# A graph network with a mixture of experts on one core: x by columns, staircases for four of 32 groups, and a unit product with a row of minus ones in the last stage

## Chip, core and metric

The kernel runs on one core of a Trainium2 chip, in one launch. The metric is the device time of that core in microseconds (us), the median of several runs. The core has five engines with one order of instructions each: TensorE (PE in the profile; PEld is its weight load), VectorE (DVE), ScalarE (ACT), GpSimd (POOL) and SyncE (SP), which here only issues transfers. Transfers run on 16 DMA engines.

## The reference

x has 6250 nodes of 256 numbers; 200,000 edges run from src to dst. With deg_out and deg_in, the numbers of edges that leave and enter a node (at least 1), the reference computes:

- h = x / sqrt(deg_out), summed over the edges into each dst, divided by sqrt(deg_in), then times W_gc plus b_gc, plus x times W_res plus b_res;
- a feed-forward network with 64 experts of which each node uses two (256 to 512 to 256, Gelu), weighted and added;
- a normalization over the nodes: subtract the mean of each column, divide by its deviation, times gamma, plus beta;
- x plus that, and a layer normalization over the 256 numbers of each node.

The first change touches deg_out and x times (W_gc, W_res), which are computed in one stage. The second touches the last two lines of this list.

## The kernel before

Nodes lie in 50 tiles of 125 rows (TP = 125, NT = 50). Edges lie in 1568 groups of 128, one edge in each partition.

**The degree stage** makes deg_out and the projections at once. Each src is split into a row (0 to 63, `row_b`) and a column (0 to 99, `col_b`). For a block of 32 groups VectorE builds one-hot tiles by comparison (`hot_pairs`, L250): `hot_row`, 64 wide, and `hot_col`, 100 wide, both bfloat16. For each group TensorE multiplies the one by the other and adds the result into the PSUM tile `degp` (L490), even groups into its upper half and odd groups into its lower half. After 49 blocks, `degp` holds the counts. They are copied to `dsb` (L518) and folded into one column per tile (`pd`, L521), from which `s_out`, one over the root of the degree, is made.

In each of the 49 turns TensorE also prepares one tile of nodes. `turned(t)` transposes the tile's two halves (L416) and ScalarE copies the result to `fT` (L419). `project(t)` multiplies `fT` by the joined weights (L425), and ScalarE copies the 512 columns to `hx` (L429). After each second tile SP writes half of `hx` to DRAM (`r_dram`, L166) and the other half into the large tile `hrow` (L164). x is loaded for two tiles at a time by `load`, two transfers for rows 0 to 111 and 112 to 124 (L164). Also in this stage SP writes zeros over `y_dram` (L453), ScalarE's queue writes zeros over `z_dram` (L507), ScalarE makes keys of the edges (`keyg`, L511), and VectorE does small pieces of the next stages (the table `masks`, L437 to L446).

The stage has its order written out by hand: each engine executes its instructions in the order of the program text. One turn issues `hot_row` and `hot_col` (two buffers each), then `turned(i + 1)`, then the 32 products, then `project(i)`, then zeros and keys. The tiles of PSUM and SBUF that are written in one turn have two buffers; the loaded x has three, of two tiles each.

**Between** lie the counting of edges per node and the sums over neighbours, the gathering of rows for sparse parts, the choice of experts, and the expert network. They aren't changed.

**The last stage** first adds the two experts' rows to x (L1528), with TensorE summing columns of x and of its squares (`pm` L1533, `pv` L1535). From these come `scale` and `less` (L1547), one row each, repeated in all partitions. `fb` holds x plus beta, loaded and added earlier. Then the 50 tiles go through in groups of 1, 2, 3, eight times 5, 3 and 1. For a group:

- `scaled`: VectorE multiplies x by `scale` (L1571) and subtracts `less` from `fb` (L1572). In a group of five it does that for three tiles only;
- `shifted`: for the other two tiles TensorE makes `fb` less `less` in PSUM, as a product of `fb` with the identity (L1564) plus a product of a row of minus ones with the row `less` (L1565). It is issued three groups ahead, with four PSUM buffers;
- `sums`: VectorE adds the two and sums each row (L1578), and scales the sums to minus means (L1580);
- `squares`: ScalarE sums the squares (L1587) and takes the root (L1589);
- `rows_out`, for the group before: VectorE finishes the factors (L1594, L1595) and makes the first output tile of a group of five (L1598), ScalarE makes the others (L1600), SP writes them out (L166).

Of the kernel before, what the change touches and what calls it, by code (L numbers as in the profile page):

```python
# [9 lines left out]
F32 = mybir.dt.float32  # L10
F32R = mybir.dt.float32r
BF16 = mybir.dt.bfloat16
# [4 lines left out]
ALU = mybir.AluOpType  # L17
# [129 lines left out]
def gnn_moe_kernel(ctx, tc, x_in, src, dst, bases, nexts, firsts, parts, lasts, W_gc, b_gc, W_res, b_res, Wg, bg, w1, b1, w2, b2,  # L147
# [68 lines left out]
    with tc.tile_pool(name="edges", bufs=1) as ep, ExitStack() as later:  # L216
# [46 lines left out]
        with tc.tile_pool(name="late", bufs=1) as lp, tc.tile_pool(name="both", bufs=2) as bp, \  # L263
# [145 lines left out]
            CG = 32  # L409
            degp = ps_deg.tile([128, 2 * NT], F32, name="degp")  # L410

            def turned(t):

                pt = ps_a.tile([128, 2, TP], F32, name="pt")
                for k in range(2):
                    T.transpose(pt[:, k, :], state[t - t % 2][:, t % 2, k * 128:(k + 1) * 128], ident[:TP, :TP])  # L416
                load(t + 4)
                state["fT", t] = ld.tile([128, 2, TP], F32, name="fT")
                S.copy(state["fT", t], pt)  # L419

            def project(t):

                pr = ps_a.tile([TP, 2 * D], F32, name="pr")
                for k in range(2):
                    T.matmul(pr, state["fT", t][:, k, :], wcat[:, k, :], start=(k == 0), stop=(k == 1))  # L425
# [30 lines left out]
            turned(0)  # L456
            for i in range(NGR // CG):
# [3 lines left out]
                hot_col = hp.tile([128, CG // 2, 2 * NT, 2], BF16, name="hot_col")  # L461
                hot_pairs(hot_col, col_b, c0, CG, 2 * NT)
# [24 lines left out]
                turned(i + 1)  # L487
                for c in range(CG):
                    r = c % 2
                    T.matmul(degp[64 * r:64 * r + 64, :], hot_row[:, c // 2, :, r],  # L490
                             hot_col[:, c // 2, :, r], start=(c0 + c < 2), stop=(c0 + c >= NGR - 2))
# [26 lines left out]
            V.tensor_copy(dsb, degp)  # L518
# [814 lines left out]
    fb = fpool.tile([TP, NT, D], F32, name="fb")  # L1333
# [4 lines left out]
    with tc.tile_pool(name="ex", bufs=2) as xp, \  # L1338
# [95 lines left out]
        def slotted():  # L1434
# [4 lines left out]
            for e in range(-1, E):  # L1439
# [20 lines left out]
                if e % 4 == 1 and e > 4 and e // 4 * 4 - 4 < NT:  # L1460
                    t0 = e // 4 * 4 - 4
                    n = min(4, NT - t0)
                    G.tensor_tensor(fb[:, t0:t0 + n, :], fb[:, t0:t0 + n, :],
# [47 lines left out]
    with tc.tile_pool(name="fin", bufs=1) as fp, tc.tile_pool(name="gat", bufs=8) as gp, \  # L1511
            tc.tile_pool(name="fl", bufs=2) as fl, \
            tc.tile_pool(name="ps_f", bufs=4, space=PSUM) as ps_f, \
# [43 lines left out]
        BY_PE = 2  # L1557

        def shifted(t0, n):
            if n < 5:  # L1560
                return
            pf = ps_f.tile([TP, BY_PE, D], F32, name="pf")
            for u in range(BY_PE):
                T.matmul(pf[:, u, :], ident[:TP, :TP], fb[:, t0 + n - BY_PE + u, :], start=True, stop=False)  # L1564
                T.matmul(pf[:, u, :], negs, less[0:1, :], start=False, stop=True)  # L1565
            part["pf", t0] = pf

        def scaled(t0, n):
            m = n - BY_PE if n == 5 else n
            xs, fs = x[:, t0:t0 + n, :], fb[:, t0:t0 + m, :]  # L1570
            V.tensor_tensor(xs, xs, scale[:, None, :].to_broadcast([TP, n, D]), ALU.mult)  # L1571
            V.tensor_tensor(fs, fs, less[:, None, :].to_broadcast([TP, m, D]), ALU.subtract)  # L1572

        def sums(t0, n):
            lm = fl.tile([TP, 5], F32, name="lm", bufs=3)
            for t in range(n):
                f = part["pf", t0][:, t - n + BY_PE, :] if n == 5 and t >= n - BY_PE else fb[:, t0 + t, :]
# [14 lines left out]
        def rows_out(t0, n):  # L1592
# [4 lines left out]
            if n == 5:  # L1597
                V.tensor_scalar(o[:, 0, :], x[:, t0, :], rs[:, 0:1], lm[:, 0:1], op0=ALU.mult, op1=ALU.add)  # L1598
            for t in range(int(n == 5), n):
# [3 lines left out]
        for g in groups[:4]:  # L1603
            shifted(*g)
        for i, g in enumerate(groups):
            if i + 4 < len(groups) and i:
                shifted(*groups[i + 3])
# [59 lines left out]
```

## Time and profile before

| | |
|---|---|
| median of the runs shown | 1617.59 us (3 runs, 1616.33 to 1620.51) |
| the profiled execution's own time | 1633.5 us |
| its span | 1631.8 us |
| mean granted clock of TensorE | 0.947 of full |
| TensorE busy | 1433.4 us (88%) |
| VectorE busy | 1077.0 us (66%) |
| ScalarE busy | 687.1 us (42%) |
| GpSimd busy | 778.6 us (48%) |
| degree products, first and last | 10.2 to 172.2 us of the span |
| last stage behind `less`, from | 1568.2 us of the span |

The profiled execution is 15.9 us longer than the median of the runs. Durations and the places in the span are read from it. In a timeline, the first two columns are the start and the length in us; "x4" says that four instructions are merged, and the brackets at the end tell how long the engine idled before and what ended that. In a table by windows, the columns are the window, its length, the busy time of PE, PEld, DVE, ACT and POOL with the number of instructions, the granted clock, the share of the DMA engines that was busy, and GB/s. In a table by groups, the numbers behind the first bar are the busy time in us and the mean ns of one.

### The profile page before, as it was taken

To read this page: it belongs to the slowest core of one execution; us is meant where nothing else is said; L and a number is where in the kernel's file an instruction comes from. 1 tells how busy PE (TensorE), PEld (TensorE's weight loads), DVE (VectorE), ACT (ScalarE), POOL (GpSimd) and SP (SyncE) were. 2 spreads that over 40 slices of the span, in tenths; PEclk is the share of its full clock that TensorE was granted. 3 is DMA by queue.
4 is the path that set the end of the run, shared out by engine and by line. 5 is a ranking of instruction groups with operands and counts; after the bars stand their busy time and mean duration, and the time that the engine had idled before them with its cause. 6 is when DMAs were issued, how large, how long until landed. Compare 5 with 4: busy or idle time off the path is not lost. (4 is left out here: it accounts for less than half of the span.)

```text
span 1631.8 us, 33437 instructions
## 1 busy us (share of the span) xinstructions
PE 1433.4 (88%) x10135; PEld 1176.7 (72%) x10135; DVE 1077.0 (66%) x2966; ACT 687.1 (42%) x1703; POOL 778.6 (48%) x878
## 2 busy tenths in 40 slices
PE   5999477888889999999999986699989999997993
PEld 3555366777778888989999975588778777775641
DVE  9999887878888878877777739533223222221897
ACT  2342543445555556555555533322122222122258
POOL 6000215666666666666666621256556666652000
PEclk9999799999999999999999997899999999999975
DMA  6889775667667777677777739488777878674924
GB/s 171 253 258 285 219 225 148 177 195 205 178 189 214 202 205 213 196 203 204 217 201 211 208 114 191 140 243 260 226 232 252 248 248 250 216 234 142 250 72 134
DMA packets 213271, 335.63 MB, mean 206 GB/s; under 512 B 23814, under 2 KB 148198, under 8 KB 213082
## 3 DMA queue, kind: packets, MB, share of 16 engines
q1 hardware_dynamic: 158294, 179.56, 38.0%
q0 software_dynamic: 47888, 146.77, 31.2%
q10 hardware_dynamic: 6900, 7.07, 1.5%
q8 instruction: 82, 1.34, 0.3%
q14 instruction: 107, 0.88, 0.2%
HBM read 253.81 MB, written 73.10 MB: 200 GB/s over the span
## 5 line engine op out<-in xcount | busy, mean ns | idle before, releaser
L568 POOL DMA_INDIRECT r<-h_dram,srcg x445 | 465.6, 1046 | 302.5 <-PE pc L651 108.8
L697 PE MATMUL sm<-hrow,counts 125*128 125x258 f32 x1500 | 496.2, 346 | 10.3 <-DVE counts L688 9.0
L671 ACT CAST counts<-pc 128x200 f32 (+7 forms) x879 | 360.9, 411 | 260.5 <-PE pc L651 135.5
L698 PE MATMUL sm<-hrow,counts 125*128 125x256 f32 x1500 | 402.4, 282 | 0.0
L651 PE MATMUL pc<-hotk,lo 128*128 128x250 bf16 (+7 forms) x1118 | 309.4, 308 | 60.7 <-DVE counts L688 22.3
L697 PEld LDWEIGHTS sm<-hrow,counts 125*128 125x128 f32 x1500 | 293.1, 195 | 35.8 <-issue 19.8
L638 DVE TENSOR_TENSOR hotk<-key,iota_h 128x800 bf16<-128x800 f16 (+4 forms) x488 | 250.8, 514 | 90.7 <-PE pc L651 56.1
L698 PEld LDWEIGHTS sm<-hrow,counts 125*128 125x128 f32 x1500 | 288.3, 192 | 1.6
L688 DVE TENSOR_TENSOR counts<-pc,counts 128x50 f32 x908 | 220.0, 242 | 57.3 <-issue 9.4
L1399 ACT ACTIVATE hT<-ph,b1c 128x112 f32<-128x112 f32 (+16 forms) x256 | 106.2, 428 | 349.1 <-PE ph L1397 183.7
L1409 PE MATMUL py<-w2s,hT 128*128 128x256 f32 (+7 forms) x992 | 240.4, 385 | 5.7 <-issue 4.0
L1397 PE MATMUL ph<-xgT,w1s 128*128 128x112 f32 (+17 forms) x1024 | 206.1, 345 | 8.7 <-ACT hT L1399 6.3
L1397 PEld LDWEIGHTS ph<-xgT,w1s 128*128 128x128 f32 x1024 | 169.4, 193 | 40.4 <-issue 12.9
L1409 PEld LDWEIGHTS py<-w2s,hT 128*128 128x128 f32 (+7 forms) x992 | 161.3, 171 | 50.2 <-issue 8.9
L1362 POOL DMA_INDIRECT y_dram<-ys,dest x124 | 119.2, 961 | 136.8 <-DVE ys L1412 70.0
L1362 POOL DMA_INDIRECT xg<-x_dram,ids x124 | 119.8, 966 | 91.8 <-DVE ids L1313 52.5
L1412 DVE TENSOR_TENSOR ys<-py,b2s 128x256 f32<-128x256 f32 (+7 forms) x124 | 51.6, 421 | 169.4 <-PE py L1409 112.4
L651 PEld LDWEIGHTS <-lo 128*128 128x128 bf16 x1118 | 101.6, 102 | 83.7 <-DVE lo L250 20.3
L573 PE MATMUL pg<-r,hot 128*128 128x258 f32 x445 | 147.3, 331 | 12.0 <-issue 7.1
L1387 DVE TENSOR_SCALAR xgT<-pte,bsum 128x112 f32<-128x112 f32 (+14 forms) x128 | 48.9, 424 | 159.7 <-PE pte L1384 65.1
L574 PE MATMUL pg<-r,hot 128*128 128x256 f32 x445 | 125.7, 282 | 0.0
L573 PEld LDWEIGHTS pg<-r,hot 128*128 128x128 f32 x445 | 85.8, 193 | 25.9 <-issue 18.6
(326 smaller groups left out, 1737.8 us busy)
## 6 DMA issues: line engine op xcount, KB each, us to landing
w1s<-in_L_gnn_w_dram SPq DMA_DIRECT2D x64, 512.0 KB
w2s<-in_L_gnn_w_dram SPq DMA_DIRECT2D x64, 512.0 KB
y_dram<-zeros SPq DMA_DIRECT2D x48, 256.0 KB
yr<-y_dram SPq DMA_DIRECT2D x25, 448.0 KB
b2s<-in_L_gnn_b_dram SPq DMA_DIRECT2D x64, 128.0 KB
r<-h_dram,srcg POOLq DMA_INDIRECT x445
h_dram<-hrow SPq DMA_DIRECT2D x5, 1344.0 KB
z_dram<-zeros ACTq DMA_DIRECT2D x7, 903.0 KB
```

The lines of the kernel that those rows point to most:

```text
L568: G.indirect_dma_start(out=f32(r[:, :2 * D]), out_offset=None, in_=h_dram[:, :], in_offset=bass.IndirectOffsetOnAxis(ap=idx, axis=0))
L573: T.matmul(pg, hot, r[:, D:], start=first, stop=False)
L574: T.matmul(pg[:, :D], hot, r[:, :D], start=False, stop=last)
L638: V.tensor_tensor(hot, pairs(key, e, n, m), iota_h[:, None, :m, :].to_broadcast([128, n // 2, m, 2]), ALU.is_equal)
L651: T.matmul(pc, los[g // PAIRS][:, r // 2, :, r % 2], hots.pop(g), start=(i == 0), stop=(i == k - 1))
L671: put = S.copy(counts[c % 2][:, :, 1:][:, :, ds(at, w - 1)], pc[:, :, 1:])
L688: add = V.tensor_tensor(to, more, f32(had), ALU.add).ins
L697: T.matmul(sm, by, hrow[:, t, D:], start=(t == 0), stop=False)
L698: T.matmul(sm[:, :D], by, hrow[:, t, :D], start=False, stop=(t == NT - 1))
L1362: w = G.indirect_dma_start(**kw)
L1397: T.matmul(ph[:, :m], w1s[:, kk, c * 128:(c + 1) * 128], xgT[:, kk, :m], start=(kk == 0), stop=(kk == 1))
L1409: T.matmul(py[:n], hT[:, c, k * 128:k * 128 + n], w2s[:, c, :], start=(c == 0), stop=(c == 3))
```

## The change

*Degree stage.* The host hands over a second copy of x, `x_cols`, laid out as pairs of tiles with columns in the partitions. `load` brings a pair with one transfer, straight as the stationary operand of the projection. `turned` is gone: no transposes, no `fT`. `load(t + 4)` is issued in `project(t)`, behind its products. `hot_col` is built for 28 of the 32 groups (CV = 28). For the other four ScalarE makes staircases: the sign of (column + 0.5 - j) for j from 0 to 100, that is 1 up to the column and -1 behind it, 101 values. Their products with `hot_row` add up in a second PSUM tile, `stp`. At the end the difference of neighbouring columns of `stp`, times 0.5, is added to `degp`: two VectorE instructions and a copy more. ScalarE makes the staircases for turn i + 1 in turn i, in front of the copy to `hx`; there are two buffers.

*Last stage.* A tile `unit` has the identity in rows 0 to 124 and minus ones in row 125. `fb` gets 128 partitions, and a transfer writes the row `less` into partition 125 of the forty tiles of the groups of five. One product of `unit` with 126 rows of `fb` then gives `fb` less `less`. It is done for all five tiles of such a group, so that `scaled` subtracts only in the small groups. `pf` has two buffers of five tiles (three PSUM banks each), and its products are issued one group ahead. VectorE makes two output tiles of a group of five instead of one, ScalarE three instead of four.

```diff
+            CV = CG - 4
+            stp = ps_deg.tile([128, 2 * NT + 1], F32, name="stp")
+            code = dp.tile([128, NGR // CG, CG - CV], F32, name="code")
             def load(t):
                 if t < NT and t % 2 == 0:
-                    state[t] = ld.tile([TP, 2, D], F32, name="f", bufs=3)
-                    node_dma(nc.sync, True, state[t], node_rows(x_in, t, 2))
+                    state[t] = ld.tile([128, 2, 2, TP], F32, name="f", bufs=3)
+                    nc.sync.dma_start(out=state[t], in_=x_cols[t // 2])
...
-            def turned(t):
-                pt = ps_a.tile([128, 2, TP], F32, name="pt")
-                for k in range(2):
-                    T.transpose(pt[:, k, :], state[t - t % 2][:, t % 2, k * 128:(k + 1) * 128], ident[:TP, :TP])
-                load(t + 4)
-                state["fT", t] = ld.tile([128, 2, TP], F32, name="fT")
-                S.copy(state["fT", t], pt)
+            def codes(i, n):
+                S.activation(code[:, i:i + n, :], col_b[:, i * CG:(i + n) * CG].rearrange("p (i c) -> p i c", c=CG)[:, :, CV:],
+                             AF.Copy, bias=0.5)
+            def stairs_of(i):
+                if i * CG == HEAD:
+                    codes(i, NGR // CG - i)
+                state["stairs", i] = hp.tile([128, CG - CV, 2 * NT + 1], BF16, name="stairs", padded_shape=[128, CG - CV, 2 * NT + 2])
+                for c in range(CG - CV):
+                    S.activation(state["stairs", i][:, c, :], iota_f[:, :2 * NT + 1], AF.Sign, scale=-1.0,
+                                 bias=code[:, i, c:c + 1])
             def project(t):
...
-                    T.matmul(pr, state["fT", t][:, k, :], wcat[:, k, :], start=(k == 0), stop=(k == 1))
+                    T.matmul(pr, state[t - t % 2][:, t % 2, k, :], wcat[:, k, :], start=(k == 0), stop=(k == 1))
+                load(t + 4)
...
-                hot_col = hp.tile([128, CG // 2, 2 * NT, 2], BF16, name="hot_col")
-                hot_pairs(hot_col, col_b, c0, CG, 2 * NT)
+                hot_col = hp.tile([128, CV // 2, 2 * NT, 2], BF16, name="hot_col")
+                hot_pairs(hot_col, col_b, c0, CV, 2 * NT)
...
-                turned(i + 1)
+                if i < NGR // CG - 1:
+                    stairs_of(i + 1)
...
+                    if c < CV:
                         T.matmul(degp[64 * r:64 * r + 64, :], hot_row[:, c // 2, :, r], hot_col[:, c // 2, :, r], ...)
+                    else:
+                        T.matmul(stp[64 * r:64 * r + 64, :], hot_row[:, c // 2, :, r], stairs[:, c - CV, :], ...)
...
-            V.tensor_copy(dsb, degp)
+            V.tensor_copy(stairs, stp)
+            V.tensor_tensor(dsb, stairs[:, :2 * NT], stairs[:, 1:], ALU.subtract)
+            V.scalar_tensor_tensor(dsb, dsb, 0.5, degp, op0=ALU.mult, op1=ALU.add)
...
-        negs = fp.tile([1, TP], F32, name="negs")
-        V.memset(negs, -1.0)
+        V.tensor_scalar(below, pidx, float(TP), -1.0, op0=ALU.is_ge, op1=ALU.mult)
+        V.tensor_scalar(unit, ident[:, :TP], below, None, op0=ALU.add)
...
+        nc.sync.dma_start(out=fb[TP:TP + 1, f0:f1, :], in_=less[0:1, None, :].to_broadcast([1, f1 - f0, D]))
         def shifted(t0, n):
...
-            pf = ps_f.tile([TP, BY_PE, D], F32, name="pf")
-            for u in range(BY_PE):
-                T.matmul(pf[:, u, :], ident[:TP, :TP], fb[:, t0 + n - BY_PE + u, :], start=True, stop=False)
-                T.matmul(pf[:, u, :], negs, less[0:1, :], start=False, stop=True)
+            pf = ps_f.tile([TP, 5, D], F32, name="pf", padded_shape=[TP, 6, D])
+            for u in range(5):
+                T.matmul(pf[:, u, :], unit[:TP + 1, :], fb[:TP + 1, t0 + u, :], start=True, stop=True)
...
-            if n == 5:
-                V.tensor_scalar(o[:, 0, :], x[:, t0, :], rs[:, 0:1], lm[:, 0:1], op0=ALU.mult, op1=ALU.add)
-            for t in range(int(n == 5), n):
+            m = 2 if n == 5 else 0
+            for t in range(m):
+                V.tensor_scalar(o[:, t, :], x[:, t0 + t, :], rs[:, t:t + 1], lm[:, t:t + 1], op0=ALU.mult, op1=ALU.add)
+            for t in range(m, n):
                 S.activation(o[:, t, :], x[:, t0 + t, :], AF.Identity, scale=rs[:, t:t + 1], bias=lm[:, t:t + 1])
```

More of the change, by code (lines that the diff above doesn't have):

```diff
@@ L146, in gnn_moe_kernel @@
 @with_exitstack
[L147 removed]
+def gnn_moe_kernel(ctx, tc, x_in, x_cols, src, dst, bases, nexts, firsts, parts, lasts, W_gc, b_gc, W_res, b_res, Wg, bg, w1, b1, w2, b2,
                    gamma, beta, out):
@@ L486, in gnn_moe_kernel @@
                     placed()
-                turned(i + 1)
+                if i < NGR // CG - 1:
+                    stairs_of(i + 1)
+                stairs = state.pop(("stairs", i))
                 for c in range(CG):
                     r = c % 2
-                    T.matmul(degp[64 * r:64 * r + 64, :], hot_row[:, c // 2, :, r],
-                             hot_col[:, c // 2, :, r], start=(c0 + c < 2), stop=(c0 + c >= NGR - 2))
+                    if c < CV:
+                        T.matmul(degp[64 * r:64 * r + 64, :], hot_row[:, c // 2, :, r],
+                                 hot_col[:, c // 2, :, r], start=(c0 + c < 2), stop=(c0 + c >= NGR - CG + CV - 2))
+                    else:
+                        T.matmul(stp[64 * r:64 * r + 64, :], hot_row[:, c // 2, :, r], stairs[:, c - CV, :],
+                                 start=(i == 0 and c < CV + 2), stop=(c0 + c >= NGR - 2))
                 if i < NGR // CG - 1:
@@ L1332, in gnn_moe_kernel @@
     fpool = ctx.enter_context(tc.tile_pool(name="fpool", bufs=1))
-    fb = fpool.tile([TP, NT, D], F32, name="fb")
+    fb = fpool.tile([128, NT, D], F32, name="fb")
     gam = fpool.tile([TP, D], F32, name="gam")
@@ L1512, in gnn_moe_kernel @@
             tc.tile_pool(name="fl", bufs=2) as fl, \
-            tc.tile_pool(name="ps_f", bufs=4, space=PSUM) as ps_f, \
+            tc.tile_pool(name="ps_f", bufs=2, space=PSUM) as ps_f, \
             tc.tile_pool(name="ps_m", bufs=1, space=PSUM) as ps_m, tc.manual_schedule():
-        negs = fp.tile([1, TP], F32, name="negs")
-        V.memset(negs, -1.0)
+        unit = fp.tile([128, TP], F32, name="unit")
+        below = fp.tile([128, 1], F32, name="below")
+        V.tensor_scalar(below, pidx, float(TP), -1.0, op0=ALU.is_ge, op1=ALU.mult)
+        V.tensor_scalar(unit, ident[:, :TP], below, None, op0=ALU.add)
         eps = fp.tile([TP, 2], F32, name="eps")
@@ L1555, in gnn_moe_kernel @@
         assert t0 == NT
-        BY_PE = 2
+        five = [g for g in groups if g[1] == 5]
+        f0, f1 = five[0][0], sum(five[-1])
+        nc.sync.dma_start(out=fb[TP:TP + 1, f0:f1, :], in_=less[0:1, None, :].to_broadcast([1, f1 - f0, D]))
         def shifted(t0, n):
@@ L1576, in sums @@
             for t in range(n):
-                f = part["pf", t0][:, t - n + BY_PE, :] if n == 5 and t >= n - BY_PE else fb[:, t0 + t, :]
+                f = part["pf", t0][:, t, :] if n == 5 else fb[:TP, t0 + t, :]
                 V.scalar_tensor_tensor(x[:, t0 + t, :], x[:, t0 + t, :], 1.0, f, op0=ALU.mult,
@@ L1641 @@
         put(name, a)
+        if name == "x":
+            put("x_cols", _np.ascontiguousarray(a.reshape(NT // 2, 2, TP, 2, 128).transpose(0, 4, 1, 3, 2)))
         if name == "dst":
```

20 lines of the change are left out of this document (11 added, 9 removed).

## The prediction

> **What bounds the kernel now.** I read the page first, for the span and for where each engine is full, then the timeline and the grouped rows of the two stages that the change touches, then their transfer shares.
>
> ```profile
> span 1631.8 us, 33437 instructions
> PE   5999477888889999999999986699989999997993
> DVE  9999887878888878877777739533223222221897
> ```
>
> A slice is 40.8 us. The degree stage is slices 1 to 4 and part of 5, and the last stage lies in the final two. The first has TensorE and VectorE both full, the second VectorE and ScalarE. The TensorE timeline of the degree stage, columns start, length, engine, line, operation:
>
> ```profile
> 31.20 1.54 PE L490 MATMUL degp<-hot_col,hot_row 128*64 128x100 bf16 x32 [7.30 <-DVE hot_col L250]
> 35.93 0.38 PE L416 MATMUL pt<-ident,f 125*128 125x125 f32 x2
> ...
> 120.08 0.38 PE L416 MATMUL pt<-ident,f 125*128 125x125 f32 x2
> 120.39 0.95 PE L490 MATMUL degp<-hot_col,hot_row 128*64 128x100 bf16 x32
> 121.27 1.98 PE L425 MATMUL pr<-wcat,fT 128*125 128x512 f32 x4
> 123.08 0.38 PE L416 MATMUL pt<-ident,f 125*128 125x125 f32 x2
> ...
> 171.19 0.38 PE L416 MATMUL pt<-ident,f 125*128 125x125 f32 x2
> ```
>
> By starts, a turn is 0.31 of transposes, 0.88 of degree products and 1.81 of projection: 3.00 us with no idle noted. From 35.93 to 171.19 there are 44 turns, 3.07 each, so nearly the whole stretch is TensorE's. VectorE, in the same stretch:
>
> ```profile
> 115.97 1.21 DVE L250 TENSOR_TENSOR hot_row<-row_b,iota 128x2048 bf16<-128x2048 bf16 x1
> 117.10 1.81 DVE L250 TENSOR_TENSOR hot_col<-col_b,iota 128x3200 bf16<-128x3200 bf16 x1
> 118.84 1.21 DVE L250 TENSOR_TENSOR hot_row<-row_b,iota 128x2048 bf16<-128x2048 bf16 x1
> ```
>
> Its turn is 1.13 + 1.74 = 2.87 us, only 0.13 shorter than TensorE's. Either engine eased alone would give 0.13 per turn; the change eases both.
>
> **The degree stage, part by part.** *Transposes.* They go, and project(t) reads x directly as columns: 0.31 per turn off TensorE, leaving 2.69. *One-hot columns.* hot_col is built for 28 of 32 groups. Between 2048 and 3200 elements the step grows from 1.13 to 1.74, so 0.53 ns an element; 400 fewer elements are 0.21, and VectorE's turn becomes 2.66. The two engines then have the same turn, and things that were hidden in VectorE's lead come out, such as this one:
>
> ```profile
> L437 DVE TENSOR_TENSOR kd<-dstf,base 128x1118 f16<-128x1118 f32 x1 | 1.3, 1317 | 0.0
> ```
>
> *Products of the last four groups.* They have 101 columns instead of 100 and go to a second PSUM tile; one column in a hundred is nothing in 0.88. *Staircases.* Four ScalarE instructions a turn replace the fT copy. ScalarE's turn now:
>
> ```profile
> 78.19 0.59 ACT L429 COPY hx<-pr 125x512 f32<-125x512 f32 x1 [1.76 <-PE pr L425]
> 78.67 0.51 ACT L511 ACTIVATE keyg<-dstf,neg 128x16 f16<-128x16 f32 x2
> 79.08 0.35 ACT L419 COPY fT<-pt 128x250 f32<-128x250 f32 x1
> ```
> ```profile
> 145.43 0.58 ACT L429 COPY hx<-pr 125x512 f32<-125x512 f32 x1 [3.25 <-PE degp L490]
> ```
>
> The nearest row with a per-partition bias and about 100 elements, and the load of an activation table:
>
> ```profile
> L1399 ACT ACTIVATE hT<-ph,b1c 128x112 f32<-128x112 f32 x52 | 18.0, 353 | 84.5 <-PE ph L1397 37.5 <-PE py L1409 20.1 <-issue 7.3
> L515 ACT ACT_TABLE_LOAD x1 | 1.3, 1283 | 0.0
> ```
>
> hx lasts 0.59 and the next starts 0.48 behind its start; the keyg pair lasts 0.51 and fT starts 0.41 behind it. So neighbours overlap by 0.10, and in a turn hx takes 0.48 and the pair 0.41. A staircase then costs between 0.25 (0.35 less 0.10) and 0.35 (no overlap); I take 0.27. ScalarE's turn is 0.48 + 0.41 + 4 x 0.27 = 1.97, at worst 2.3: it fits in 2.69. The Trainium skill, "ScalarE: Activation LUTs", section "What ACT_TABLE_LOAD costs", puts an instruction with a bias pointer at about 280 ns + 0.833 ns an element with 93 ns of overlap; that estimate is 0.27 for 101 elements, and the trace agrees with its 0.353 for 112 within 0.02.
>
> What is lost is slack. The hx copy of turn i stands in ScalarE's order before the staircases for turn i+2. Now a late hx delays only fT, which is wanted by a projection a whole turn later. Afterwards ScalarE's 1.97 begins when a projection ends, so the staircases end about 2.0 us into a turn, and they are wanted at 2.69 + 0.77 (28/32 of the 0.88): 1.5 to spare. The row at 145.43 waited 3.25; a turn of 3.00 less hx (0.48) and fT (0.35) leaves 2.17, so it was 1.1 late. TensorE did not stop for it and would not afterwards, but at twice that it would. Such a copy waits for hx to be written out, so the transfers decide how often. Their share of the 16 DMA engines (columns at the end: clock, share, GB/s):
>
> ```profile
> 42.00:172.00 130.00, 127.77 (x1625) 75.04 (x1625) 124.94 (x93) 45.52 (x121) 0.62 (x1) 1.00 0.88 266
> 100.00:112.00 12.00, 12.00 (x160) 7.01 (x156) 12.00 (x10) 3.40 (x9) 0.00 (x0) 1.00 0.93 274
> 1522.00:1554.00 32.00, 31.36 (x125) 21.20 (x125) 28.52 (x63) 9.49 (x16) 0.00 (x0) 1.00 1.05 251
> ```
>
> The same bytes in 2.69/3.00 of the time need a share of 0.98. The last row holds 1.05 over 32 us, so it is possible, but the mean leaves little. On SP's queue the two x transfers per pair of turns become one, with 128 rows of 2000 B for 250 of 1 KB; bytes do not change, and I cost this at nothing (it can only shorten SP's issue, which hides beside TensorE). load(t+4) moves behind project(t), one turn later, and still leads its use by four turns, 10.8 us.
>
> Sum of the stage. The start: VectorE is the limit up to turn 3 (the 7.30 wait for hot_col at 31.20), so four shorter hot_cols bring 0.8, or 0.2 if the split that follows turn 2 then waits for srcf. The 44 turns: 44 x 0.31 = 13.6 at best. Of that I give back 2.0 for VectorE's side jobs (1.3 in the row above, and others of its kind) and late hx copies; the bounds are 0 and 9.7, the latter from the first rival below. The end:
>
> ```profile
> 172.49 0.26 DVE L518 COPY dsb<-degp 128x100 f32<-128x100 f32 x1 [3.05 <-PE degp L490]
> ```
>
> This copy becomes a copy, a subtraction and a multiply-add of the same size, two more of 0.2 to 0.26 on the path to s_out: +0.45. So -0.8 - 13.6 + 2.0 + 0.45 = -12.0 us. Nothing between the stages starts at a time of its own: VectorE stood idle 3.05 for degp here, so what follows moves forward with it.
>
> **The last stage.** VectorE's timeline of one group of five:
>
> ```profile
> 1590.25 1.49 DVE L1571 TENSOR_TENSOR x<-x,scale 125x1280 f32<-125x1280 f32 x1
> 1591.65 0.95 DVE L1572 TENSOR_TENSOR fb<-fb,less 125x768 f32<-125x768 f32 x1
> 1592.71 0.43 DVE L1578 SCALAR_TENSOR_TENSOR x<-x,fb 125x256 f32<-125x256 f32 x1
> ...
> 1595.05 0.41 DVE L1598 TENSOR_SCALAR o<-x,ssq,lm 125x256 f32<-125x256 f32 x1
> 1595.38 1.49 DVE L1571 TENSOR_TENSOR x<-x,scale 125x1280 f32<-125x1280 f32 x1
> ```
>
> The group takes 5.13. The subtraction of three tiles goes: without it the first sum could start at 1590.25 + 1.49 + 0.11 (the gap seen behind the subtraction) = 1591.85 instead of 1592.71, so 0.86. A second output tile comes: 0.33. Net 0.53, and 8 groups make 4.2. ScalarE:
>
> ```profile
> 1592.43 2.06 ACT L1600 ACTIVATE o<-x,lm,ssq 125x256 f32<-125x256 f32 x4
> 1594.76 0.51 ACT L1587 ACTIVATE sq<-x,lm 125x256 f32<-125x256 f32 x1 [0.27 <-DVE lm L1580]
> ```
>
> Its group is 5.13 too, 0.27 of it waiting, and loses one of four output tiles, 0.49: 4.38 against VectorE's 4.60, so VectorE stays the limit. Behind the last group ScalarE alone sets the end, and two sets of outputs there lose a tile each: up to 1.0, of which I take 0.5. Together -4.7, bounds -4.2 and -5.2.
>
> TensorE must deliver five products a group in 4.60. Its rows: a tile by identity and the row of minus ones alternating as now, and dense products with 125 rows at the start of this stage, before and after the clock comes up.
>
> ```profile
> 1568.29 1.21 PE L1565 MATMUL pf<-less,negs 1*125 1x256 f32 x2 [3.59 <-DVE less L1547]
> 1569.43 1.22 PE L1564 MATMUL pf<-fb,ident 125*125 125x256 f32 x2
> ```
> ```profile
> 1512.81 1.91 PE L1535 MATMUL pv<-sq,ones 125*125 125x256 f32 x4
> 1514.52 1.91 PE L1533 MATMUL pm<-x,ones 125*125 125x256 f32 x4
> ```
> ```profile
> 1518.34 1.03 PE L1535 MATMUL pv<-sq,ones 125*125 125x256 f32 x4
> ```
> ```profile
> 1572.00:1576.00 4.00, 4.00 (x8) 1.68 (x8) 3.90 (x13) 2.52 (x9) 0.00 (x0) 0.50 0.11 32
> ```
>
> A product costs 1.14 now (clock 0.50), 0.855 dense at the low clock (1.71 for two), and by lengths 1.03/1.91 of that, 0.46, at the high one. The new products are all alike, 126 rows, as the dense ones: 4.3 per group at worst, below 4.60. The Trainium skill, "TensorE: Matmul & The Clock Gate", Part 1, says some 3.4 us of sustained work brings the full clock; the dense rows agree (low at 1512.81, high at 1518.34), the row of 1572 to 1576 does not: TensorE is busy 4.00 of 4.00 and stays at 0.50. By the page five products would be 2.2, by the worst row 5.7. The row of -less reaches partition 125 by a transfer behind less (1568.2); even 2.5 us of it and 4.3 of products end at 1575.1, before group 3 needs them near 1576.8.
>
> **Sum.** -12.0 - 4.7 = -16.7. Against the profiled execution (1633.5 us, span 1631.8) that is 1616.8; the runs have a median of 1617.59, 15.9 below it, and with the same difference they give **1601 us**. The stretch alone: 1597 (nothing given back, -5.2) to 1609.
>
> **The rivals.**
>
> *Transfers set the turn.* For it: 0.88 mean share, late hx copies; against it: the 1.05 row. At the 274 GB/s of 100 to 112, the stretch from 42 to 172 (266 x 130 = 34.6 MB) takes 126.1 us, only 3.9 less, 9.7 short of 13.6. Then -0.8 - 3.9 + 0.45 - 4.7 = -9.0: 1608.6. Chance 0.18.
>
> *TensorE sets the last stage.* If the clock stays at 0.50 and a product stays at 1.14, five are 5.7 against 5.13: 8 x 0.57 = +4.6 in place of -4.7, in all -7.4: 1610. For it, the row at 0.50 with TensorE busy throughout; against it, the dense rows. Chance 0.08. The clock page's rule speaks against this rival.
>
> *The gain of the degree stage does not arrive,* because something up to 970 us waits for what does not move. The chain of waits does not reach back to the degree stage, so it cannot exclude it. Only -4.7: 1613. Chance 0.06.
>
> *Slower: the activation table is swapped each turn.* If the staircase's function and the copies share no table, each turn has two loads of 1.28 in ScalarE's order: 1.97 + 2.57 = 4.5 us, 49 x 1.5 = +74 against 3.00; with -4.7: 1687. It decides once ScalarE's turn passes 3.00. Against it: hx copies run both before and behind the load at L515 with no other load between. Chance 0.03. The Trainium skill, "ScalarE: Activation LUTs", section "Table sets: the hidden batching unit", lists cheap functions as being in every set, and does not name Sign.
>
> *It doesn't do what it says:* VectorE's side jobs make it the limit from the start and the transposes were free. But TensorE ran without idle at 3.00; 0.02, near 1606.
>
> **How the numbers follow.** The forecast has 0.60, and the rest of the probability, 0.03, is for what I have not seen. The forecast's own range is 1597 to 1606. To leave out no more than 0.2 the range takes in the first two rivals and a little below: **1595 to 1611**. A change of less than 0.3% (4.9 us, so 1612.7 to 1622.4) can't be told from none here. Faster: forecast, both first rivals, the fifth: 0.88. Same: the third and a part of the unseen, 0.07. Slower: 0.05.
>
> **What would show it.** Right: starts of the degree products 2.65 to 2.8 apart, hot_col near 1.6, staircases 0.35 each and no table load before the square root; in the last stage a group of 4.6 and products of 0.46 to 0.86. Wrong: TensorE waiting for staircases, hx copies waiting for hrow in most turns, DMA share near 1 with turns of 2.9, or sums waiting for pf.

## The result, and the profile after

| | before | after |
|---|---|---|
| median of the timed runs beside each other | 1619.02 us | 1605.49 us |
| profiled execution, and its span | 1633.5, 1631.8 us | 1602.28, 1600.6 us |
| dsb complete (end of the degree stage) | 172.75 us | 162.95 us |
| from less to the end | 64.0 us | 58.0 us |

The changed kernel takes 0.9914 of the time, with a 95% interval from 0.9891 to 0.9936: 13.9 us less on 1619.02, between 10.4 and 17.6. The forecast was 16.6 less on 1617.6 (0.990), with a range from 1595 to 1611.

The page's slices of the changed kernel:

```profile
span 1600.6 us, 33304 instructions
PE   5999477888889999999999986699989999999773
DVE  8999888888887888877777739532323332222797
ACT  3676544345565655565555533322222222222248
```

TensorE and VectorE are still full in slices 2 to 4, and ScalarE has become busier there. TensorE's timeline in the degree stage (start, length, engine, line, operation):

```profile
127.77 0.85 PE L503 MATMUL degp<-hot_col,hot_row 128*64 128x100 bf16 x28
128.46 0.26 PE L506 MATMUL stp<-stairs,hot_row 128*64 128x101 bf16 x4
128.65 1.98 PE L433 MATMUL pr<-wcat,f 128*125 128x512 f32 x4
130.56 0.84 PE L503 MATMUL degp<-hot_col,hot_row 128*64 128x100 bf16 x28
...
158.31 0.84 PE L503 MATMUL degp<-hot_col,hot_row 128*64 128x100 bf16 x28
158.99 0.25 PE L506 MATMUL stp<-stairs,hot_row 128*64 128x101 bf16 x4
161.08 0.84 PE L503 MATMUL degp<-hot_col,hot_row 128*64 128x100 bf16 x28
```

A turn is 2.77 to 2.79 us by starts (127.77 to 130.56, 158.31 to 161.08), 2.775 on the mean, not the 2.69 of the forecast. The projection begins 0.88 behind the degree products, as before, but the projection keeps the next products waiting 1.91 (128.65 to 130.56), where it kept the transposes waiting 1.81 before. VectorE and ScalarE in the same stretch:

```profile
119.12 1.60 DVE L250 TENSOR_TENSOR hot_col<-col_b,iota 128x2800 bf16<-128x2800 bf16 x1
120.64 1.21 DVE L250 TENSOR_TENSOR hot_row<-row_b,iota 128x2048 bf16<-128x2048 bf16 x1
121.78 1.60 DVE L250 TENSOR_TENSOR hot_col<-col_b,iota 128x2800 bf16<-128x2800 bf16 x1
```
```profile
100.60 1.19 ACT L426 ACTIVATE stairs<-iota_f,code 128x101 bf16<-128x101 f32 x4
103.82 0.59 ACT L438 COPY hx<-pr 125x512 f32<-125x512 f32 x1 [2.03 <-PE stp L506]
```

VectorE's turn is 2.66 (119.12 to 121.78), as worked out, and the four staircases last 1.19 together, close to 4 x 0.27 + 0.10. The stage's window (busy time of PE, PEld, DVE, ACT and POOL, then clock, share of the 16 DMA engines, GB/s):

```profile
40.00:160.00 120.00, 117.62 (x1518) 62.46 (x1517) 117.16 (x94) 78.45 (x246) 0.62 (x1) 1.00 0.94 289
```

The same window of the kernel before has a share of 0.87 and 264 GB/s: the transfers followed the shorter turn.

The last stage, first VectorE's group of five and then TensorE's products:

```profile
1567.68 1.48 DVE L1592 TENSOR_TENSOR x<-x,scale 125x1280 f32<-125x1280 f32 x1
1569.30 0.42 DVE L1601 SCALAR_TENSOR_TENSOR x<-x,pf 125x256 f32<-125x256 f32 x1
...
1571.63 0.73 DVE L1622 TENSOR_SCALAR o<-x,ssq,lm 125x256 f32<-125x256 f32 x2
1572.28 1.49 DVE L1592 TENSOR_TENSOR x<-x,scale 125x1280 f32<-125x1280 f32 x1
```
```profile
1546.42 6.78 PE L1587 MATMUL pf<-fb,unit 126*125 126x256 f32 x20 [7.39 <-DMA fb<-less]
1553.55 2.42 PE L1587 MATMUL pf<-fb,unit 126*125 126x256 f32 x10 [0.34 <-DVE x L1601]
...
1571.15 4.21 PE L1587 MATMUL pf<-fb,unit 126*125 126x256 f32 x10 [1.32 <-DVE x L1601]
1575.75 2.42 PE L1587 MATMUL pf<-fb,unit 126*125 126x256 f32 x10 [0.39 <-DVE x L1601]
```

The group is 4.60, to the hundredth what was forecast, and every batch of products but the first waits for VectorE to free its PSUM tile, so TensorE is not the limit. The first batch waits for the row `less` in partition 125 of `fb`: less is done at 1543.00 and the products begin at 1546.42, so the row lands within 3.4 us and not within 2.5.

**A trap in these two profiles.** Their spans differ by 31.2 us, over twice what the medians do. The degree stage gives 9.8 of that and the last 6.0; the other 15.4 lie between the stages, which the change does not touch. The stretch from dsb to less, in the kernel before and in the changed one:

```profile
172.75:1567.81 1395.06, 1245.53 (x8208) 1071.92 (x8208) 861.49 (x2649) 580.79 (x1391) 751.62 (x783) 0.96 0.72 206
```
```profile
163.00:1542.58 1379.58, 1240.02 (x8206) 1070.48 (x8206) 861.15 (x2650) 581.79 (x1391) 756.06 (x783) 0.97 0.72 208
```

The kernel before was therefore profiled again. (The first profile's own time, 1633.5 us, also lies outside the timed runs beside it, 1616.3 to 1621.5.)

### The profile page after: what moved, and what is told of

Same layout as the page of the kernel before. It is cut to its first block, busy times and chain, and to the rows that moved or that the text cites. A ratio compares the mean times of both kernels' runs of the same rounds, so it can differ in the third digit from the quotient of the medians.

```text
span 1600.6 us, 33304 instructions
## 1 busy us (share of the span) xinstructions
PE 1404.0 (88%) x10051; PEld 1162.5 (73%) x10051; DVE 1062.1 (66%) x2969; ACT 724.2 (45%) x1843; POOL 779.7 (49%) x878
## 5 line engine op out<-in xcount | busy, mean ns | idle before, releaser
L587 POOL DMA_INDIRECT r<-h_dram,srcg x445 | 470.8, 1058 | 289.1 <-issue 102.8
L433 PE MATMUL pr<-wcat,f 128*125 128x512 f32 x200 | 102.1, 635 | 0.1
```

Source lines behind the costliest of these rows:

```text
L587: G.indirect_dma_start(out=f32(r[:, :2 * D]), out_offset=None, in_=h_dram[:, :], in_offset=bass.IndirectOffsetOnAxis(ap=idx, axis=0))
```

## The experiments

Each ratio is the time over that of the kernel before in the same set of runs on one chip. "dsb at" is the end of the degree stage, "the stretch between" goes from there to less.

**The kernel before, once more** (no edit).

> The kernel before, unchanged, with one more profile: how far the same program's stretch from dsb to the first scaled varies from one execution to another. Theory A (variation of single executions): its span comes out some us away from the 1631.8 us of the first profile, between 1605 and 1632, the difference lying in that stretch, and dsb done at 172 to 173 us, from the first scaled to the end 63 to 64 us as in the first. Theory B (the middle of the changed kernel is really shorter): span 1628 to 1635 again, with 1393 to 1397 us in that stretch.

Measured: 1571.68 us, span 1569.9, in a set of runs (chip 11) where the kernel before has a median of 1569.96 us. Its degree stage ends at 172.1 us and less to the end takes 64.0, as in the first profile, but the stretch between, which has the same instructions, is 61 us shorter:

```profile
172.20:1505.95 1333.75, 1229.69 (x8208) 1063.66 (x8208) 862.74 (x2648) 587.12 (x1391) 748.35 (x783) 0.97 0.76 216
```

Neither theory had such a span, and the record names no chip for the first two profiles, so this run alone shows only that the stretch moves by more than 15.4 us without an edit. Kernels of one set settle it: on chip 11 the stretch takes 1333.8 here and 1329.4 to 1333.6 in the three other kernels, on chip 9 (the set of the changed kernel's second profile) 1392.1 in the kernel before with one product changed (minus identity, below) and 1389.6 in the changed kernel. So the 15.4 us are no gain of the change, in the main; differences of up to 5 us remain within a set. All the following comparisons use ratios of runs on one chip, and from the profiles only the two stretches that the change touches.

**The degree stage alone.** The kernel before with the hunks of the degree stage (columns of x and staircases); the last stage is the old one.

> The kernel before with the degree stage of the changed kernel alone (x by columns, staircases for 4 of 32 groups); the last stage is the old one. Theory A (the two halves add up, and the 1395.4 against 1380.0 us that the two profiles show between the stages is the variation of single executions): dsb is done about 9.8 us earlier than before, at 162.5 to 163.5 us; about 1609 us, ratio 0.993 to 0.995; the stretch from dsb to the first scaled is anywhere from 1380 to 1396 and follows the granted clock. Theory B (the degree stage's new form shortens what stands behind it as well, for instance by when its tiles come free): the stretch from dsb to the first scaled is again near 1380 here and near 1395 where the degree stage is the old one, and the ratio is that of the whole change, 0.991 or less.

Ratio 0.9923 (0.9908 to 0.9939), dsb at 163.7 us, less to the end 63.9, the stretch between 1329.4 us. That is just beyond theory A's range, and the interval touches theory B's 0.991. The time is 12.1 us less (9.6 to 14.4), but the stage gave 8.4 against the kernel before in the same set and the last stage 0.1. The stretch between is 4.4 us shorter than there, but only 0.8 shorter than in the next run, which has the old degree stage. So a shortening by 15 us, as theory B has it, is not there; whether a few us of this gain arise behind the stage stays open.

**The last stage alone.** The kernel before with only the hunks of the last stage.

> The kernel before with the last stage of the changed kernel alone (one product with a unit tile and a row of minus ones, two output tiles on VectorE); the degree stage is the old one. Theory A (the halves add up): from the first scaled to the end 57.5 to 58 us against 63.6 before, so -6 us, about 1613 us, ratio 0.995 to 0.998; dsb done at 172 to 173 us as before. Theory B (the last stage brings more than its own stretch, because the features stand in 128 partitions and the middle's writes of them go otherwise): the stretch from dsb to the first scaled falls to about 1380 and the time to about 1606 or less. Theory C (the last stage's gain is made up by the profile alone, the late row of less and the products take it back): ratio 0.999 to 1.001.

Ratio 0.9962 (0.9947 to 0.9978), which is the 6.0 us that the profile shows from less to the end (58.0 against 64.0). dsb at 170.5 us, 1.5 earlier than expected with the old stage; the stretch between 1330.2. Theory A. The product of the two ratios is 0.9885.

**The changed kernel again** (no edit).

> The changed kernel once more, beside a new set of runs of the kernel before. Theory A (the halves add up: the degree stage alone measured 0.9923 and the last stage alone 0.9962, product 0.9885): ratio 0.987 to 0.991, with dsb done at 163 to 164 us and 58 us from less to the end. Theory B (part of the degree stage's gain is lost in the middle whenever both halves are in): ratio 0.991 to 0.994 with the same two stretches.

Ratio 0.9898 (0.9876 to 0.9920), dsb at 165.3 us, less to the end 58.0. The halves add up within the intervals; this one and that of the first comparison, 0.9914, overlap. The value is theory A's, but both intervals reach into theory B's 0.991 to 0.994, so a loss of a few us isn't excluded. dsb is 2.3 us later than in the first profile, and a part of that has a row:

```profile
157.75 1.01 PE L506 MATMUL stp<-stairs,hot_row 128*64 128x101 bf16 x4 [0.88 <-ACT stairs L426]
```

Here TensorE did wait for ScalarE, once: an hx copy had waited 4.59 us for a transfer out of hx (to hrow), and the staircases behind it came late. The turn took 4.58 us (156.02 to 160.61), 1.81 more than the others; 0.88 of that is the wait in the row, and most of the rest are the four products, which last 1.01 instead of 0.26.

**Columns without staircases.**

```
-            CV = CG - 4
+            CV = CG
...
-            V.tensor_copy(stairs, stp)
-            V.tensor_tensor(dsb, stairs[:, :2 * NT], stairs[:, 1:], ALU.subtract)
-            V.scalar_tensor_tensor(dsb, dsb, 0.5, degp, op0=ALU.mult, op1=ALU.add)
+            V.tensor_copy(dsb, degp)
```

> The changed kernel without the staircases: VectorE makes the columns of all 32 groups again, x still comes by columns, and there are no steps to be added up at the end. Theory A (the turn is set by the later of TensorE, 2.775 us, and VectorE, 2.66 us with 28 columns): VectorE's turn becomes 2.66 + 4/28 x 1.53 = 2.88 us, above TensorE's, so VectorE sets the turn, its side jobs then add to the stage in full, and the degree stage ends 44 x 0.10 = 4.4 to 7 us later less 0.6 us for the shorter tail; about 1609 to 1612 us. Theory B (TensorE sets the turn whatever VectorE makes): turn 2.775 as it is, dsb done 0.6 us earlier, about 1605 us. Theory C (the staircases themselves hold TensorE up): turn below 2.775 and a time below 1604 us.

Ratio 0.9921 (0.9902 to 0.9939); dsb at 167.9 us. VectorE then sets the turn:

```profile
157.93 1.21 DVE L250 TENSOR_TENSOR hot_row<-row_b,iota 128x2048 bf16<-128x2048 bf16 x1
159.07 1.80 DVE L250 TENSOR_TENSOR hot_col<-col_b,iota 128x3200 bf16<-128x3200 bf16 x1
160.81 1.21 DVE L250 TENSOR_TENSOR hot_row<-row_b,iota 128x2048 bf16<-128x2048 bf16 x1
```

2.88 from one to the next without a gap, and TensorE's products start 2.87 apart. dsb is 2.6 to 5.0 us later than in the four profiles with both parts of the stage, as theory A has it; in the total time the difference from the changed kernel is inside the intervals.

**Staircases without columns.** The kernel before, with stairs_of and CV = CG - 4; x still comes by rows and is transposed.

> The kernel before with the staircases alone: 4 of 32 groups go to ScalarE, x still comes by rows and is transposed on TensorE, the last stage is the old one. Theory A (two engines stood level before, TensorE at 3.00 and VectorE at 2.88 us a turn, so relief of VectorE alone gives nothing): turn 2.98 to 3.01 us, dsb done between 1 us earlier and 1 us later than before (172.2 us in the last but one look), ratio 0.999 to 1.001. Theory B (VectorE was the limit and its side jobs were paid in full): turn 2.80 to 2.85 us, dsb 7 us or more earlier, ratio 0.995 or less.

Ratio 0.9981 (0.9966 to 0.9996), dsb at 171.9 us:

```profile
122.08 0.85 PE L514 MATMUL degp<-hot_col,hot_row 128*64 128x100 bf16 x28
122.75 0.27 PE L517 MATMUL stp<-stairs,hot_row 128*64 128x101 bf16 x4
122.95 1.98 PE L443 MATMUL pr<-wcat,fT 128*125 128x512 f32 x4
124.77 0.38 PE L434 MATMUL pt<-ident,f 125*128 125x125 f32 x2
125.08 0.85 PE L514 MATMUL degp<-hot_col,hot_row 128*64 128x100 bf16 x28
```

The turn is 3.00 as before. Theory A: with TensorE at 3.00, relief of VectorE shows almost nowhere. (The ratio is a little under the forecast's 0.999; a degree stage that ends where it ended doesn't explain these 3 us, and they stay open, as do the few us of the degree stage alone.) So the dsb times are: neither part 170.5 to 172.8 in four profiles, staircases 171.9, columns 167.9, both 162.9 to 165.3. Each part alone gives at most half, since the other engine is next.

**Six staircases instead of four** (CV = CG - 6).

> The changed kernel with the staircases of 6 of 32 groups on ScalarE instead of 4 (VectorE makes 26). Theory A (TensorE sets the turn now, 2.775 us, and VectorE at 2.66 us only catches up after each side job): from 60 to 160 us the turn stays at 2.77 to 2.79 us; VectorE's own turn becomes 2.66 - 2/28 x 1.53 = 2.55 us, so the side jobs are absorbed sooner, dsb done 0 to 1.5 us earlier than in the changed kernel beside it, and no difference in time that can be told (ratio to the changed kernel 0.999 to 1.001). Theory B (VectorE still sets the turn): 44 x 0.11 = 4.8 us less. Theory C (ScalarE becomes late: 6 staircases at 0.29 us and two copies at 0.59 us are 2.9 us a turn, over TensorE's 2.775): turn 2.9 us and about 5 us more.

Ratio 0.9910 (0.9888 to 0.9932) against 0.9898 for the changed kernel beside it; dsb at 165.3 us in both. VectorE now idles: in the window from 40 to 160 us it is busy 111.3 us, against 115.8 with four, and TensorE's turn stays at 2.77. Theory A: VectorE is no longer the limit. Theory C, a late ScalarE, shows in four turns: 3.87, 3.60 and 3.12 in a row, and 3.73 later, with staircase products of up to 1.38 instead of 0.31. The first of them begins with an hx copy that waited 1.99 for a transfer; then six staircases a turn and two further instructions of 1.13 and 1.14 keep ScalarE late. So the equal dsb is the sum of a gain and of this loss.

**Each projection in two halves**, one after the 16th and one after the 32nd degree product:

```
+                    if c == 16 and i < NGR // CG - 1:
+                        half_of(i, 0)
...
-                    project(i)
+                    project(i, 1)
```

> The changed kernel with each projection's two halves apart: the first half of the inner dimension after the 16th of the 32 degree products of the turn, the second behind the 32nd. The same products, but TensorE changes between the f32 projection and the bf16 degree products four times a turn instead of two. Theory A (a change of the kind of product costs about 0.1 us a time: in the changed kernel a turn is 0.86 us of degree products and 1.71 us of projection passes, and 0.20 us are left over at the two changes): turn 2.775 + 0.20 = 2.97 us, dsb done about 8 us later, ratio about 5 thousandths worse than the changed kernel. Theory B (the 0.20 us belong to the wait for the projection's PSUM tile or the start of a turn): turn 2.77 to 2.80 us, no change.

Ratio 1.0005 (0.9985 to 1.0025), 1.1 hundredths worse than the changed kernel beside it; dsb at 178.2 us, 12.9 later:

```profile
123.69 0.56 PE L511 MATMUL degp<-hot_col,hot_row 128*64 128x100 bf16 x16
124.18 1.12 PE L433 MATMUL pr<-wcat,f 128*125 128x512 f32 x2
125.23 0.47 PE L511 MATMUL degp<-hot_col,hot_row 128*64 128x100 bf16 x12
125.54 0.26 PE L514 MATMUL stp<-stairs,hot_row 128*64 128x101 bf16 x4
125.72 1.12 PE L433 MATMUL pr<-wcat,f 128*125 128x512 f32 x2
126.78 0.57 PE L511 MATMUL degp<-hot_col,hot_row 128*64 128x100 bf16 x16
```

The turn is 3.09 (123.69 to 126.78), 0.31 more than 2.78 for the same products. Two passes hold the degree products back 1.05 us here, four held them back 1.91 above; so a pass costs 0.43, and 0.19 to 0.20 are paid once, each time the f32 projection gives way to bf16. The rest of the 0.31 is on the way back: 16 products last 0.49 instead of half of 0.88. Theory A, at one and a half times its size. Type, shape and weights change together at these places, so the runs don't show which of them costs it.

**The projections of two turns together**, to halve these changes:

```
-                load(t + 4)
...
-                if i < NGR // CG - 1:
-                    project(i)
+                load(i + 4)
+                if i % 2:
+                    project(i - 1)
+                    project(i)
```

> The changed kernel with the projections of two turns one after the other behind the degree products of the second (64 bf16 products, then 8 f32 passes): TensorE changes kind twice in two turns instead of four times, the products are the same. Theory A (one change there and back costs 0.31 us, as the split projection showed): TensorE needs 2 x 2.775 - 0.31 = 5.24 us for two turns, 2.62 each, and VectorE with 2.66 us is the limit again; dsb done 3 to 5 us earlier than in the changed kernel, ratio to the kernel before 0.986 to 0.989. Theory B (transfers are next: the DMA engines were busy 0.97 of the stage at 2.78 us a turn): the turn stays above 2.69 us and TensorE waits for f. Theory C (VectorE gets its buffers back later, since two turns of products run at a time): VectorE idle over 3 us between 60 and 160 us, dsb no earlier than in the changed kernel.

and the same with six staircases:

> As the paired projections, and with staircases for 6 of 32 groups, so that VectorE's turn is 2.55 us. Theory A (TensorE sets it at 2.62 us a turn, VectorE's side jobs find room): dsb done 5 to 7 us earlier than in the changed kernel, ratio to the kernel before 0.985 to 0.987, the best of all. Theory B (the DMA engines are full): no turn below 2.69 us, dsb as with 4 staircases. Theory C (buffers return late): VectorE idles, no earlier than with 4 staircases.

Ratios 0.9965 (0.9951 to 0.9980) and 1.0020 (1.0004 to 1.0037), dsb at 173.3 and 184.4 us: both worse than the changed kernel (0.9914 and 0.9898). Theory C's two signs are there: from 60 to 160 us VectorE idles 7.6 us with four staircases and 18.8 with six, against 1.3 and 2.8 in the changed kernel's two profiles, and dsb is later. But no theory had ScalarE's part in it. TensorE and ScalarE with six staircases:

```profile
133.37 0.81 PE L502 MATMUL degp<-hot_col,hot_row 128*64 128x100 bf16 x26
134.01 0.30 PE L505 MATMUL stp<-stairs,hot_row 128*64 128x101 bf16 x6
134.14 0.77 PE L502 MATMUL degp<-hot_col,hot_row 128*64 128x100 bf16 x26
134.74 1.20 PE L505 MATMUL stp<-stairs,hot_row 128*64 128x101 bf16 x6
135.88 3.70 PE L433 MATMUL pr<-wcat,f 128*125 128x512 f32 x8
139.50 0.80 PE L502 MATMUL degp<-hot_col,hot_row 128*64 128x100 bf16 x26
```
```profile
133.48 0.59 ACT L437 COPY hx<-pr 125x512 f32<-125x512 f32 x1 [1.13 <-PE pr L433]
133.96 3.35 ACT L426 ACTIVATE stairs<-iota_f,code 128x101 bf16<-128x101 f32 x12
```

The second set of staircase products lasts 1.20 instead of 0.30. ScalarE does its copies and staircases in program order. The second copy of the pair waits for the second projection (to 133.48), and all twelve staircases of the next two turns queue behind it; TensorE needs the first six from 134.74 on, and the sixth is made at about 133.96 + 6 x 0.28 = 135.6. The products go on as the tiles arrive: each lasts 0.21 as ever, but they start 0.27 apart, and the row, which merges them, shows the wait as length. Eight passes hold the next products back 3.62 (135.88 to 139.50), 8 x 0.43 + 0.18, so the change of kind is indeed paid half as often; but a pair of turns takes 6.13 us, against 2 x 2.78. With four staircases the same delay is smaller (0.49 for the second set, 5.59 us a pair), and waits for hot_col of 6.4 us in all come on top, since VectorE waits for its buffers, as theory C has it. Staircases made a pair ahead of the copies might take ScalarE's delay away; that was not tried.

**Minus identity instead of minus ones**, in the kernel before:

```
-        negs = fp.tile([1, TP], F32, name="negs")
-        V.memset(negs, -1.0)
+        negs = fp.tile([TP, TP], F32, name="negs")
+        V.tensor_scalar(negs, ident[:TP, :TP], -1.0, None, op0=ALU.mult)
...
-                T.matmul(pf[:, u, :], negs, less[0:1, :], start=False, stop=True)
+                T.matmul(pf[:, u, :], negs, less, start=False, stop=True)
```

> The kernel before with the second product of each pair over all 125 rows (minus identity times less) instead of over one row of minus ones; same numbers out. In the last stage of the kernel before TensorE was busy without a gap at a granted clock of 0.50, in that of the changed kernel it reached 1.00 within 8 us. Theory A (products that use one row of 128 don't count as load, and the clock stays low because of them): the granted clock goes to 1.00 within 5 to 10 us of the first pair, the mean of these products from 0.63 us to 0.40 us; group on VectorE 5.13 us as before, so the time is unchanged. Theory B (the clock answers to something else, such as the alternation of the two sets of weights): 0.50 from 1572 us on (as before), mean 0.63 us.

1629.10 us in a single execution, less to the end 64.0: no difference in time, as VectorE sets the group. But the products:

```profile
1563.88 1.21 PE L1565 MATMUL pf<-less,negs 125*125 125x256 f32 x2 [3.60 <-DVE less L1547]
...
1566.59 0.97 PE L1564 MATMUL pf<-fb,ident 125*125 125x256 f32 x2
1567.39 0.60 PE L1565 MATMUL pf<-less,negs 125*125 125x256 f32 x2
1567.82 0.59 PE L1564 MATMUL pf<-fb,ident 125*125 125x256 f32 x2
```

From 1.0 to 1.2 they fall to 0.59 (0.43 from start to start) at 1567.39, 3.5 us after the first. With one row in every second product they stayed at 1.21 for as long as they ran, with TensorE never idle. The granted clock is 0.95 from 1567 to 1570, where it was 0.50 in the kernel before. Theory A: what kept the clock down was the one-row product; the two sets of weights alternate here too. Later in this run, where TensorE pauses 1.4 to 2.9 us before each batch, the clock falls again (0.50 from 1584 to 1596).

**One output tile on VectorE instead of two** (m = 1 if n == 5 else 0), in the changed kernel.

> The changed kernel with one of a group's five output tiles on VectorE instead of two, as before the change; ScalarE makes four. Theory A (VectorE and ScalarE stand close in the last stage, 4.60 us a group on VectorE): VectorE's group falls to 4.60 - 0.27 = 4.33 us, ScalarE's rises to about 4.87 us and sets the group; 8 groups x 0.27 = 2.2 us longer from less to the end, 60.2 against 58.0 us. Theory B (VectorE is the limit with room on ScalarE): the group falls towards 4.4 us and the stretch to 56.5 us.

Ratio 0.9921 (0.9904 to 0.9938); less to the end 60.4 us against 58.0. The group starts at 4.28 and then settles at 4.75, with VectorE waiting for an output buffer to be written out, which cannot start before ScalarE has made its tiles:

```profile
1518.06 0.41 DVE L1622 TENSOR_SCALAR o<-x,ssq,lm 125x256 f32<-125x256 f32 x1 [0.60 <-DMA out_dram<-o]
```

Theory A: ScalarE would set the group. Without the move of the second output tile the stretch still falls from 64.0 to 60.4; the move brings the other 2.4 of the 6.0 us.

## Why the prediction was right, and where it was off

**The forecast as a whole** held: both stages gained, the parts add up, and the two comparisons (0.9914 and 0.9898) are near its 0.990. Its own sum, -12.0 and -4.7, was off by terms that partly cancel: the rows show -8.0 and -6.0, 14.0 us in all. The first comparison gives 13.9 us; that the second gives 16.7, the forecast's own sum, is luck as far as the rows show. Two slips changed nothing: by its own terms (-0.8 - 13.6 + 0.45 - 5.2) its lower end is 1598.4 and not 1597, and five products at 0.46 are 2.3 us and not 2.2.

**The start, -0.8: not there.** hot_col is shorter, but turn 4 starts at 34.5 to 35.5 us in four profiles with the new stage and at 34.3 to 36.2 in four with the old, 35.1 and 35.0 on the mean. A preparation step of VectorE (row_b, 128 x 128) lasted 0.34 us in three of the four old ones and 1.52 in the first profile; in the four new ones it lasted 1.31 to 1.52. Each long one ended at 6.55, just behind a run of GpSimd memsets that starts at 5.0 and ends at 6.5, and the short ones began before these. Where the step was long, turn 4 starts at 36.2 in the old stage and at 34.5 to 35.5 in the new: a gain is there, and the long step took it back. That the memsets held it up was not tested, nor why the new stage always began it behind them. The first profile, from which I worked, had lost that time already; its wait of 7.30 for hot_col was no fixed property.

**The transposes, 44 x 0.31: the mis-sized term.** This is the step that was most in error. It read the 0.31 between a transpose and the degree products as the price of the transposes. The turn fell by 0.225 (3.00 to 2.775), so 9.9 us instead of 13.6. The f32 transposes stood between the f32 projection and the bf16 products; without them the projection holds the next products back 0.10 longer. The split projection shows such a cost by itself, about 0.20 each time.

**Given back, 2.0: measured 1.2.** Over the 44 turns, four profiles of each kind average 135.4 us before (44 x 3.00 + 3.4) and 126.7 after (44 x 2.775 + 4.6). It came from where the step put it, pauses for hot_col and late copies. The claim that a late copy would not stop TensorE failed in two of the four new profiles: one turn took 1.81 more in the changed kernel's second, and one 0.93 more in the run with one output tile.

**The end of the stage, +0.45: measured 0.6.** Three VectorE instructions take 0.86 instead of 0.26. Together: +0.1 - 8.7 + 0.6 = -8.0 against -12.0, and dsb in four profiles of each kind lies 8.0 us earlier on the mean (163.7 and 171.7).

**The last stage, -4.7: measured -6.0.** The group went from 5.13 to 4.60 as worked out, and the first step of the groups fell by 0.85 (4.66 to 3.81) where 0.53 was counted. The other seven steps gave 3.7. The tail is the term that was too small: from the last scaling to the end 12.0 us became 10.0, and the step ahead of it took 0.6 more (0.33 for the second output tile, the rest a wait of 0.31), so 1.4. ScalarE had run behind VectorE there, as VectorE's last wait for it shows, before and after:

```profile
1624.76 0.16 DVE L1594 RECIPROCAL ssq<-ssq 125x1 f32<-125x1 f32 x1 [2.41 <-ACT ssq L1589]
```
```profile
1593.63 0.16 DVE L1617 RECIPROCAL ssq<-ssq 125x1 f32<-125x1 f32 x1 [1.29 <-ACT ssq L1612]
```

So the output tiles taken from ScalarE count on the path; with one of them given back (the last run) the tail is 11.95 us again. The step had priced this at 0.5, and its upper bound was 1.0.

**The prices.** VectorE's 2.66, ScalarE's staircases at 0.27 (1.19 for four) and the lack of table loads (none between 1.3 and 161.8 us) are right. The estimate that the prediction took from the Trainium skill, "ScalarE: Activation LUTs", section "What ACT_TABLE_LOAD costs", agrees with that 1.19. The landing of the row less took 3.4 us instead of 2.5 and cost nothing: the first products still came before their sums.

**The rivals.** *Transfers set the turn:* false here. The turn is steady at 2.775 with the DMA engines at 0.94, and TensorE waits for no transfer in the 44 turns of the changed kernel's first profile (for x once, 0.42, in the degree stage alone); the forecast's share of 0.98 assumed the shorter turn. *TensorE sets the last stage:* false; products took 0.48 to 0.84 on the mean of a batch, and its cause, a clock that never left 0.50, went with the one-row products. The slowest batch, 4.21, is what the prediction had at worst (4.3) and fits into the group of 4.60. *The degree gain does not arrive:* false by the run with that stage alone. *A table swapped each turn:* false, the staircases stand between copies without a load. *Transposes were free:* false, but columns alone give only half, since VectorE with 2.88 is right behind.

**The clock rule against the row.** The Trainium skill, "TensorE: Matmul & The Clock Gate", Part 1, and the row at 0.50 were both right: with 125 rows in every product the clock came up in 3.5 us, and with one row in every second product it did not in 35 us. What the rule says of sustained work holds here for products of 125 or 126 rows.

## What to carry to other kernels

Where two engines stand within 5% of each other, price each edit by the gap to the next engine, and ease both for the whole gain: columns alone ended the stage 4 us earlier, staircases alone not at all, both 8. A gap between two kinds of products belongs to the pair and not to the one that ends it: removing a step between f32 and bf16 products returns less than its place in the timeline. Before work is regrouped on one engine, look at what another engine does in program order behind it; a copy that waits can hold back work that was ready.

## What the runs showed of the hardware

- From f32 passes to bf16 products TensorE lost about 0.20 us each time: 1.05, 1.91 and 3.62 us for two, four and eight passes of 0.43.
- Products of 125 rows and of one row in turn did not bring the clock up in 35 us of uninterrupted work; the same kernel with 125 rows in both reached 0.59 us a product, from 1.21, after 3.5 us.
- TensorE waiting for input that comes piece by piece can appear as a longer row of products (1.20 against 0.30) with no wait noted: the gaps between the products are only 0.06 us each.
- The stretch between the two stages has the same instructions in all these kernels. It took 1395 and 1380 us in the first two profiles, 1390 to 1394 on chip 9, 1329 to 1334 on chip 11 and 1329 to 1332 on chip 14; of two profiles only the stretches that an edit touches may be compared.
